# ScalarE writes the negated row maxima into the score banks ahead of the matmuls, in place of a fourth matmul pass

## The chip, the core and the metric

The kernel runs on one core of a Trainium2 chip. The metric is device time in microseconds (us), the median of three executions. The core has a TensorE (PE in the profile; PEld is its weight load), a VectorE (DVE), a ScalarE (ACT), a GpSimd (POOL) and a SyncE (SP), which here issues every DMA. Each engine works through its own instructions in program order and waits for the others through semaphores. Matmuls write into eight PSUM banks of 128 partitions by 512 fp32; VectorE and ScalarE read and write them as well.

## The reference

Four sequences of 1024 tokens, width 128, pass through half a mixture-of-experts FFN, an attention layer, and half the same FFN again:

```python
x = x + 0.5 * ffn(layernorm(x), ...)
x = x + attn(layernorm(x), ...)      # 16 heads of 64: q, k, v from two latents, rotary embedding,
                                     # softmax(q k^T / 8) v, output projection, residual
x = x + 0.5 * ffn(layernorm(x), ...)
```

The change touches the attention alone: for each query the scores against all 1024 keys, minus the query's largest score, go through an exponential.

## The kernel before

**Units.** The attention is cut into 64 units (`NUNIT`): two heads (`hh` is 0 or 1) by 512 queries each, 16 units to a sequence. The profile shows them as a stretch from 220 to 1457 us, one every 19 us or so. Inside a unit there are eight slots `s`, one for each tile of 128 keys. A score tile (`s`, `hh`) has the keys on the partitions and the 512 queries along the bank. The two heads lie on partitions 0 to 63 and 64 to 127, so that a matmul of one head runs beside a matmul of the other.

**Scores** (`score`, L938 and L942). Each tile is the sum of four matmuls `k`: high by high, high by low and low by high parts of K and Q, and as the last one `one_row` by `maxr`, an outer product that adds the negated maximum of each query, since the query lies along the bank and ScalarE's bias can't be used. Then ScalarE takes the exponential into `p` (L942) and GpSimd adds the tiles up for the denominator (`accumulate`, L954). Six banks go round: tile (`s`, `hh`) has bank number `(2*(s % 8) + hh) % 6` of psS0 to psS3, psC, psX.

**Maxima** (`passA`, L912 and L913). The maxima are taken 15 slots ahead from a single high-by-high product, 16 matmuls a unit into psA0 and psA1, each reduced by VectorE. `MAXIMA` says ahead of which score matmul of its head each of the first six pairs stands. `max_row` turns the 128x8 result into a row through DRAM: one DMA writes it, a second reads it back element by element into `maxr`, both on SP's queue.

**Order of a unit's program.** First `rows(0)` and `rows(1)`, interleaved one by one: 32 score matmuls of each head with the maxima between them, then the output projection of an earlier unit (`outp`, L997, a bank for each head: `bankO`) and the rotary step's three matmuls for each half (L797, banks `rope_banks`). After the rows, in this order:

- `scale`: ScalarE multiplies the two output banks by the reciprocal denominators, eight instructions (L1012).
- `den(U - 1)`: eight small matmuls (L974) and a ScalarE copy `dsb` (L976).
- `rope(U, "vector")`: VectorE's rotary arithmetic (L810 to L816); then the ScalarE casts to `hi_r` (L820).
- `add(1)` on VectorE: an output bank is added to X (L1006).
- `rope(U, "low")`: two VectorE subtractions (L823).
- `add(0)`, in the place "late": the other output bank.
- `values`: 32 matmuls into psC (L962), and the ScalarE copy `osb` (L965).

Between the values, `step(...)` runs pieces of the preparation of later blocks ("flows": the norms of coming attention blocks and of the second FFN, ScalarE's at L252, L691 and L695). After the values `step(PE)` may run a PE piece, such as the transposes L707 and L759 of a tile just normed, into psX (and in the first eight units a second one into psS3). Some forty of the 64 units have such pieces on ScalarE or PE. The next unit's scores begin behind them.

Rotary work runs nine units ahead (`NROPE`), so that units 55 to 63 have none.

Of the kernel before, what the change touches and what calls it, by code (L numbers as in the profile page):

```python
# [29 lines left out]
NGRP = NSLOT // 4  # L30
NUNIT = NSLOT // 8
PBUFS = 10
MAXIMA = ((2, 8, 13, 19, 24, 29), (0, 5, 11, 16, 21, 27))
OTHER, VECTOR, PE, NEVER, SCALAR, POOL = 0, 1, 2, 3, 4, 5
NROPE = 9
ACTS = (4, 6, 7)
# [11 lines left out]
class Kernel:  # L48
# [10 lines left out]
    def setup(self):  # L59
        nc, tc, ctx, ins = self.nc, self.tc, self.ctx, self.ins  # L60
        pool = lambda name, bufs, **k: ctx.enter_context(tc.tile_pool(name=name, bufs=bufs, **k))
        self.const = const = pool("const", 1)
        self.dram = pool("dram", 1, space=DRAM)
        self.small = pool("small", 2)
        self.prep = pool("prep", 1)

        bank = lambda name: pool(name, 1, space=PSUM).tile([128, 512], F32, name=name)
        self.psA, self.psS, self.psC, self.psX = [bank(f"ps_a{i}") for i in range(2)], [bank(f"ps_s{i}") for i in range(4)], bank("psc"), bank("psx")
        self.rest, self.nrest, self.slot, self.bankO = self.psA, 0, -NSLOT, None
        self.rope_banks = self.psA  # L70
# [12 lines left out]
        nc.scalar.activation(silu, silu, AF.Silu)  # L83
        self.consts = const.tile([128, 4], F32, name="consts")
        for i, c in enumerate((0.5, -CENTER, 1.0, EPS)):
            nc.gpsimd.memset(self.consts[:, i:i + 1], c)
        self.neghalf = const.tile([128, TPB], F32, name="neghalf")
        nc.gpsimd.memset(self.neghalf, -0.5)
        self.ones = const.tile([128, 32], F32, name="ones")
        nc.gpsimd.memset(self.ones, 1.0)  # L90

        self.one_row = const.tile([128, 128], F32R, name="one_row")
        nc.gpsimd.memset(self.f(self.one_row), 0.0)
        for hh in range(2):
            nc.gpsimd.memset(self.f(self.one_row[64 * hh:64 * hh + 1, :]), 1.0)
        self.maxr = [const.tile([128, 512], F32R, name=f"maxr{i}") for i in range(2)]
        for t in self.maxr:
            nc.gpsimd.memset(self.f(t), 0.0)

        self.table = const.tile([128, 3, S], F32, name="table")  # L100
# [818 lines left out]

    def max_row(self, U, m):  # L920
        nc = self.nc
        d = self.dram.tile([128, 8], F32, name=f"d3_{U % 4}")
        self.dma(out=d, in_=m)
        self.dma(out=self.maxr[U % 2][0:128:64, :].rearrange("h (q p) -> h q p", p=128), in_=d.rearrange("p (h q) -> h q p", h=2))

    def score(self, s, hh, k):


        nc = self.nc
        U, c = divmod(s, 8)  # L930
# [5 lines left out]
        ps = (self.psS + [self.psC, self.psX])[(2 * (s % 8) + hh) % 6]  # L936
        w, x = ((K[r, 0, ks], Q[r, 0, qs]), (K[r, 0, ks], Q[r, 1, qs]), (K[r, 1, ks], Q[r, 0, qs]), (self.one_row[r, :], self.maxr[U % 2][r, :]))[k]
        nc.tensor.matmul(ps, w, x, start=k == 0, stop=k == 3)  # L938
        if k == 3:
            if hh == 0:  # L940
                self.p_of[s] = self.pp.tile([128, 2, 512], F32, name="p")
            nc.scalar.activation(self.p_of[s][:, hh, :], ps, AF.Exp, scale=0.125)  # L942
            if hh == 1:
                self.accumulate(s)

    def accumulate(self, s):
# [20 lines left out]
    def den(self, U):  # L967

        nc = self.nc
        pd = self.psS[3]  # L970
        parts = [self.p_of[8 * U + c] for c in range(8 - direct(U), 8)] + [self.acc_of[U]]
        for k, part in enumerate(parts):
            for n in range(4):
                nc.tensor.matmul(pd[32 * n:32 * n + 32, 0:256], self.ones, part[:, n // 2, 256 * (n % 2):256 * (n % 2) + 256], start=k == 0, stop=k == len(parts) - 1)  # L974
        dsb = self.op1.tile([128, 256], F32, name="dsb")
        nc.scalar.copy(dsb, pd[:, 0:256])  # L976
        dT = self.ms.tile([128, 8], F32, name="dT")

        d1 = self.dram.tile([4, 256], F32, name=f"d1_{U % 4}")
        nc.sync.dma_start(out=d1, in_=dsb[0:128:32, :])  # L980
        g = 2 * U + 4
        self.at(g + (U == NUNIT - 1), lambda: nc.sync.dma_start(out=dT, in_=d1.rearrange("(h x) (y p) -> p (h x y)", x=2, p=128)), "mid")
        self.at(g + (2 if U == NUNIT - 1 else 1), lambda: self.outp(U, self.osb_of.pop(U), dT), "side")

    def outp(self, U, osb, dT):
# [8 lines left out]

        def mm(i, hh):
            r = slice(64 * hh, 64 * hh + 64)
            nc.tensor.matmul(po[hh][:, i * 128:(i + 1) * 128], osb[r, i * 128:(i + 1) * 128], self.G[r, j, :], start=True, stop=True)  # L997

        for hh in range(2):
            self.halves[hh] += [lambda i=i, hh=hh: mm(i, hh) for i in range(4)]  # L1000
# [11 lines left out]
                    nc.scalar.activation(po[hh][:, c], po[hh][:, c], AF.Identity, scale=rT[:, 4 * hh + i:4 * hh + i + 1])  # L1012

        self.at(self.group, scale, "scale")
        self.at(self.group, lambda: add(1))
        self.at(self.group, lambda: add(0), "late")

    def run(self):
        nc, tc = self.nc, self.tc
# [103 lines left out]
        for _ in streams[2].pop() if streams[2] else ():  # L1123
            pass
        assert not (streams[0] or streams[2])
        self.rest, self.rope_banks, self.bankO = [self.psX, self.psS[3]], self.psS[1:3], [self.psX, self.psS[0]]
        flows, needs, blocks = [], {}, list(range(1, B))
        self.attending = True

# [27 lines left out]
        for U in range(NUNIT):  # L1157
# [4 lines left out]

            def rows(hh):
                maxima = lambda i: self.passA(s0 + AHEAD + i, hh) if s0 + AHEAD + i < NSLOT else None
                for n in range(32):
                    if n in MAXIMA[hh]:
                        yield lambda n=n: maxima(MAXIMA[hh].index(n))
                    yield lambda n=n: self.score(s0 + n // 4, hh, n % 4)
                if hh == 1:
                    yield lambda: maxima(6)  # L1170
                for n, fn in enumerate(side[hh]):
                    if hh == 0 and n == 2:
                        yield lambda: maxima(6)
                    yield fn
                if hh == 0 and len(side[hh]) < 3:
                    yield lambda: maxima(6)
                yield lambda: maxima(7)

            for n, pair in enumerate(zip_longest(rows(0), rows(1))):
# [24 lines left out]
                if n == 32:  # L1204
# [32 lines left out]
        with ExitStack() as ctx:  # L1237
# [6 lines left out]
            g = self.ffn_pre(self.prep, (6, 7), x_of, self.wts2[:, 3].rearrange("p e t -> p t e"), rows=3)  # L1244

            def bg2(n):
                for place in ("mid", "side", "scale", "end", "late"):
# [62 lines left out]
```

## Time and profile before

| | us |
|---|---|
| median of 3 runs | 1624.37 (1622.91 to 1625.29) |
| profiled execution | 1621.56 |
| its span | 1619.7 |
| PE busy in the span | 1570.5 |
| POOL busy | 1378.8 |
| DVE busy | 1298.5 |
| ACT busy | 1115.2 |

The granted TensorE clock was 0.995. A group's row gives the line, the engine, what it writes and reads, the shape, the count, then the busy time and the mean duration of one in ns, and last the engine's idle time ahead of it. A row of the timeline gives the start, the length of a merged run, the engine and line, the count, and the idle time ahead of it with what ended it. Banks have no numbers there: psS0 to psS3 are all `ps_s`.

### The profile page before, as it was taken

The page shows a single profiled execution, that of the slowest core. Times are in us where ns is not written, and L with a number is a line of the kernel's source. Part 1 is how long each engine was busy: PE and PEld are TensorE (multiplying, and loading weights), DVE is VectorE, ACT ScalarE, POOL GpSimd, SP SyncE. Part 2 cuts the span into 40 slices and gives each one's busy share as a digit, 9 for nine tenths or more (in the row PEclk, how much of TensorE's full clock was granted, in tenths as well). Part 3 has the DMA queues.
Part 4 walks back from the last instruction along what each step waited for, and adds up shares of the span by engine and source line. Part 5 has one row for each costly group of instructions (what it writes and reads, how often), then busy time and mean ns, then how long its engine had stood idle before and what let it go on. Part 6 is the DMA issues. An engine that isn't in the chain of part 4 may idle for free.

```text
span 1619.7 us, 31073 instructions
## 1 busy us (share of the span) xinstructions
PE 1570.5 (97%) x10924; PEld 1054.0 (65%) x10924; DVE 1298.5 (80%) x2308; ACT 1115.2 (69%) x2488; POOL 1378.8 (85%) x820
## 2 busy tenths in 40 slices
PE   7998999999999999999999999999999999999998
PEld 5876766666666666566666666666666666556776
DVE  6566678898888889988888898889888866616897
ACT  4675667768777777777777777777677676665554
POOL 5678889989888889988989998989998898994676
PEclk9999999999999999999999999999999999999999
DMA  7025565565555555555555555655665532025543
GB/s 230 1 66 157 156 170 144 133 156 132 144 132 131 153 149 138 150 139 138 132 144 144 133 142 135 166 151 139 152 153 137 130 93 55 2 93 148 140 132 102
DMA packets 241148, 212.27 MB, mean 131 GB/s; under 512 B 157664, under 2 KB 170592, under 8 KB 240224
## 3 DMA queue, kind: packets, MB, share of 16 engines
q1 hardware_dynamic: 240992, 210.28, 50.0%
q8 instruction: 87, 1.43, 0.4%
q14 instruction: 69, 0.57, 0.1%
HBM read 130.39 MB, written 79.82 MB: 130 GB/s over the span
## 4 chain that ended last, share of the span: by engine, by line
PE 82%; DVE 6%; ACT 4%; POOL 3%; DMA 2%; issue 2%; SPq 1%; POOLq 0%; DVEq 0%; ACTq 0%
PE psc L962 25%; PE ps_s L938 21%; PE ps_a L912 8%; PE psc L938 4%; PE ps_s L463 3%; PE psx L938 3%; PE ps_s L543 3%; PE ps_s L797 2%; PE ps_s L997 2%; PE ps_s L974 2%; DVE m L913 2%; PE psx L498 2%; PE psc L434 1%; PE psx L997 1%; PE psc L543 1%
## 5 line engine op out<-in xcount | busy, mean ns | idle before, releaser
L954 POOL TENSOR_TENSOR acc<-acc,p 128x1024 f32<-128x1024 f32 x381 | 907.0, 2381 | 29.8
L913 DVE TENSOR_REDUCE m<-ps_a 128x1 f32<-128x512 f32 x1024 | 671.2, 685 | 161.9 <-PE ps_a L912 138.5
L942 ACT ACTIVATE p<-ps_s 128x512 f32<-128x512 f32 x768 | 411.5, 601 | 66.5 <-PE ps_s L938 42.7
L962 PE MATMUL psc<-p,ckn 128*64 128x512 f32 x2048 | 453.6, 595 | 0.0
L938 PE MATMUL ps_s<-QT,KT 64*128 64x512 f32 x2304 | 420.1, 394 | 0.3 <-DVE C_a L718 0.3
L912 PE MATMUL ps_a<-KT,QT 64*128 64x512 f32 x1024 | 390.1, 413 | 7.6 <-DVE m L913 5.8
L962 PEld LDWEIGHTS psc<-p,ckn 128*64 128x64 f32 x2048 | 141.4, 137 | 282.0 <-issue 282.0
L938 PEld LDWEIGHTS ps_s<-QT,KT 64*128 64x128 f32 x2304 | 284.3, 184 | 57.4 <-DVE X L1006 17.0
L954 POOL TENSOR_TENSOR acc<-p 128x1024 f32<-128x1024 f32 x64 | 153.8, 2403 | 86.8 <-ACT p L942 84.5
L912 PEld LDWEIGHTS ps_a<-KT,QT 64*128 64x128 f32 x1024 | 174.1, 184 | 43.4 <-DVE m L913 17.3
L938 PE MATMUL ps_s<-maxr,one_row 64*128 64x512 f32 x768 | 194.5, 392 | 0.0
L820 ACT CAST hi_r<-ps_s 128x512 fp32r<-128x512 f32 x110 | 64.5, 587 | 122.7 <-DVE ps_s L815 119.5
L938 PE MATMUL psx<-QT,KT 64*128 64x512 f32 x384 | 119.1, 390 | 0.0
L965 ACT COPY osb<-psc 128x512 f32<-128x512 f32 x64 | 37.3, 583 | 111.5 <-PE psc L962 111.5
L938 PE MATMUL psc<-QT,KT 64*128 64x512 f32 x384 | 109.2, 390 | 0.0
L938 PEld LDWEIGHTS ps_s<-maxr,one_row 64*128 64x128 f32 x768 | 102.4, 184 | 10.0
L551 POOL TENSOR_TENSOR p<-eo,p 128x512 fp32r<-128x512 f32 x42 | 62.7, 1499 | 41.5 <-ACT p L550 32.6
L1012 ACT ACTIVATE psx<-psx,rT 128x128 f32<-128x128 f32 x248 | 85.2, 344 | 17.5 <-ACT p L942 11.5
L447 POOL TENSOR_TENSOR X<-X,dtmp 128x512 f32<-128x512 f32 x54 | 69.2, 1281 | 31.7 <-ACT dtmp L446 30.6
L1012 ACT ACTIVATE ps_s<-ps_s,rT 128x128 f32<-128x128 f32 x248 | 84.3, 340 | 6.0
L942 ACT ACTIVATE p<-psc 128x512 f32<-128x512 f32 x128 | 77.4, 605 | 6.7 <-PE ps_a L912 3.3
L942 ACT ACTIVATE p<-psx 128x512 f32<-128x512 f32 x128 | 77.9, 608 | 0.0
(268 smaller groups left out, 2664.0 us busy)
## 6 DMA issues: line engine op xcount, KB each, us to landing
C_l<-cs SPq DMA_DIRECT2D x128, 256.0 KB
QT<-qs SPq DMA_DIRECT2D x256, 128.0 KB
KT<-ks SPq DMA_DIRECT2D x256, 128.0 KB
qs<-hi_r SPq DMA_DIRECT2D x32, 512.0 KB
qs<-eo SPq DMA_DIRECT2D x32, 512.0 KB
ks<-hi_r SPq DMA_DIRECT2D x32, 512.0 KB
ks<-eo SPq DMA_DIRECT2D x32, 512.0 KB
rt<-wt SPq DMA_DIRECT2D x52, 256.0 KB
```

What stands on the lines that cost most here:

```text
L447: nc.gpsimd.tensor_tensor(X[:, t:t + 4, :], X[:, t:t + 4, :], tmp, ALU.add)
L463: nc.tensor.matmul(p, w[:, a, e, :], xs[:, c, :], start=k == 0, stop=k == 2)
L543: nc.tensor.matmul(p, w[:, a, e, :], xs[:, c, :], start=k == 0, stop=k == 2)
L551: (nc.gpsimd if m < N - 1 else nc.vector).tensor_tensor(sh[:, 1, :], hp, self.f(sh[:, 0, :]), ALU.subtract)
L820: nc.scalar.copy(w["hi"][:, k, :], w["ps"][k])
L912: nc.tensor.matmul(self.psA[hh], self.QT[P % 3][r, 0, q0:q0 + 128], self.KT[P % 3][r, 0, kk * 512:kk * 512 + 512], start=True, stop=True)
L913: nc.vector.tensor_reduce(m[0][:, hh, qb, kk:kk + 1], self.psA[hh], AX.X, ALU.max)
L938: nc.tensor.matmul(ps, w, x, start=k == 0, stop=k == 3)
L942: nc.scalar.activation(self.p_of[s][:, hh, :], ps, AF.Exp, scale=0.125)
L954: nc.gpsimd.tensor_tensor(acc, self.p_of[s - 1] if c == 1 else acc, self.p_of[s], ALU.add)
L962: nc.tensor.matmul(self.psC[64 * hh:64 * hh + 64, :], self.ckn[b % 2][:, c, :], self.p_of[s][:, hh, :], start=c == 0, stop=c == 7)
L1012: nc.scalar.activation(po[hh][:, c], po[hh][:, c], AF.Identity, scale=rT[:, 4 * hh + i:4 * hh + i + 1])
```

## The change

Three parts belong together.

1. `max_row` writes the row to DRAM already transposed (two rows of 512), reads it into `maxr` with contiguous rows, and, from unit 1 on, also reads it broadcast over all 128 partitions into a new tile `maxb` (512 KB).
2. At the end of each unit, behind `rope(U, "low")`, `fill(U + 1)` has ScalarE copy `maxb` into the banks of the next unit's tiles (0, 0), (0, 1), (1, 0), and, from unit 9 on, (1, 1). These tiles then have three matmuls, the first of which adds to the bank; the fourth is left out. `MAXIMA` is dealt anew for the shorter rows.
3. Banks: the output projection goes from psX and psS0 to psS0 and psS1, the rotary step from psS1 and psS2 to psS2 and psS3, the denominator from psS3 to psX. Both adds now stand ahead of `rope(U, "low")`. In an output bank only the first of four quarter matmuls has the start flag.

```diff
-MAXIMA = ((2, 8, 13, 19, 24, 29), (0, 5, 11, 16, 21, 27))
+MAXIMA = ((2, 7, 13, 18, 23, 28), (0, 5, 10, 15, 20, 25))
...
     def max_row(self, U, m):
         nc = self.nc
-        d = self.dram.tile([128, 8], F32, name=f"d3_{U % 4}")
-        self.dma(out=d, in_=m)
-        self.dma(out=self.maxr[U % 2][0:128:64, :].rearrange("h (q p) -> h q p", p=128), in_=d.rearrange("p (h q) -> h q p", h=2))
+        d = self.dram.tile([2, 512], F32, name=f"d3_{U % 4}")
+        self.dma(out=d.rearrange("h (q p) -> p h q", p=128), in_=m.rearrange("p (h q) -> p h q", h=2))
+        self.dma(out=self.maxr[U % 2][0:128:64, :], in_=d)
+        if U:
+            self.nc.sync.dma_start(out=self.maxb.rearrange("p h q -> p (h q)"), in_=d.rearrange("h q -> (h q)").unsqueeze(0).to_broadcast([128, 1024]))
+
+    def bank(self, s, hh):
+        return (self.psS + [self.psC, self.psX])[(2 * (s % 8) + hh) % 6]
+
+    def fill(self, U):
+        for s, hh in ((0, 0), (0, 1), (1, 0)) + (((1, 1),) if U > 8 else ()):
+            self.nc.scalar.copy(self.bank(s, hh), self.maxb[:, hh, :])
+            self.filled.add((8 * U + s, hh))
...
-        nc.tensor.matmul(ps, w, x, start=k == 0, stop=k == 3)
-        if k == 3:
-            if hh == 0:
+        nc.tensor.matmul(ps, w, x, start=k == 0 and not filled, stop=k == last, skip_group_check=filled)
+        if k == last:
+            second = s in self.p_of
+            if not second:
...
-        pd = self.psS[3]
+        pd = self.psX
...
-            nc.tensor.matmul(po[hh][:, i * 128:(i + 1) * 128], osb[r, i * 128:(i + 1) * 128], self.G[r, j, :], start=True, stop=True)
+            nc.tensor.matmul(po[hh][:, i * 128:(i + 1) * 128], osb[r, i * 128:(i + 1) * 128], self.G[r, j, :], start=i == 0, stop=True, skip_group_check=i > 0)
...
-        self.at(self.group, lambda: add(1))
-        self.at(self.group, lambda: add(0), "late")
+        self.at(self.group, lambda: [add(hh) for hh in range(2)])
...
-        self.rest, self.rope_banks, self.bankO = [self.psX, self.psS[3]], self.psS[1:3], [self.psX, self.psS[0]]
+        self.rest, self.rope_banks, self.bankO = [self.psX, self.psS[3]], self.psS[2:4], self.psS[0:2]
...
             rope(U, "low")
-            self.run_later(2 * U + 1, "late")
+            if U + 1 < NUNIT:
+                self.fill(U + 1)
             rope(U, "end")
```

More of the change, by code (lines that the diff above doesn't have):

```diff
@@ L98, in setup @@
             nc.gpsimd.memset(self.f(t), 0.0)
+        self.maxb = const.tile([128, 2, 512], F32, name="maxb")
+        self.filled = set()
         self.table = const.tile([128, 3, S], F32, name="table")
@@ L935, in score @@
         Q, K = self.QT[P % 3], self.KT[P % 3]
-        ps = (self.psS + [self.psC, self.psX])[(2 * (s % 8) + hh) % 6]
+        ps = self.bank(s, hh)
+        filled = (s, hh) in self.filled
+        last = 2 if filled else 3
         w, x = ((K[r, 0, ks], Q[r, 0, qs]), (K[r, 0, ks], Q[r, 1, qs]), (K[r, 1, ks], Q[r, 0, qs]), (self.one_row[r, :], self.maxr[U % 2][r, :]))[k]
-        nc.tensor.matmul(ps, w, x, start=k == 0, stop=k == 3)
-        if k == 3:
-            if hh == 0:
+        nc.tensor.matmul(ps, w, x, start=k == 0 and not filled, stop=k == last, skip_group_check=filled)
+        if k == last:
+            second = s in self.p_of
+            if not second:
                 self.p_of[s] = self.pp.tile([128, 2, 512], F32, name="p")
             nc.scalar.activation(self.p_of[s][:, hh, :], ps, AF.Exp, scale=0.125)
-            if hh == 1:
+            if second:
                 self.accumulate(s)
@@ L1164, in rows @@
                 maxima = lambda i: self.passA(s0 + AHEAD + i, hh) if s0 + AHEAD + i < NSLOT else None
-                for n in range(32):
+                steps = [(s, k) for s in range(s0, s0 + 8) for k in range(3 if (s, hh) in self.filled else 4)]
+                for n, (s, k) in enumerate(steps):
                     if n in MAXIMA[hh]:
                         yield lambda n=n: maxima(MAXIMA[hh].index(n))
-                    yield lambda n=n: self.score(s0 + n // 4, hh, n % 4)
+                    yield lambda s=s, k=k: self.score(s, hh, k)
                 if hh == 1:
@@ L1203, in run @@
                     self.run_later(2 * U + 1, "mid")
-                if n == 32:
+                if n == 31:
                     self.run_later(2 * U + 1, "side")
@@ L1246, in bg2 @@
             def bg2(n):
-                for place in ("mid", "side", "scale", "end", "late"):
+                for place in ("mid", "side", "scale", "end"):
                     self.run_later(NGRP + 1 + n, place)
```

## The prediction

> **What bounds the kernel now.** I read the page first: busy shares, then the chain that ended last, then the groups.
>
> ```profile
> PE 1570.5 (97%) x10924; PEld 1054.0 (65%) x10924; DVE 1298.5 (80%) x2308; ACT 1115.2 (69%) x2488; POOL 1378.8 (85%) x820
> ...
> PE 82%; DVE 6%; ACT 4%; POOL 3%; DMA 2%; issue 2%; SPq 1%; POOLq 0%; DVEq 0%; ACTq 0%
> ...
> L938 PE MATMUL ps_s<-maxr,one_row 64*128 64x512 f32 x768 | 194.5, 392 | 0.0
> ...
> L965 ACT COPY osb<-psc 128x512 f32<-128x512 f32 x64 | 37.3, 583 | 111.5 <-PE psc L962 111.5
> ```
>
> PE bounds the span, and the maxima matmuls to be cut stand on it. ScalarE idles for 111.5 us ahead of `osb`: the tail of a unit, where the fills go. So I read that tail in the timeline, engine by engine, in a unit without flow pieces:
>
> ```profile
> 1182.32 2.24 ACT L942 ACTIVATE p<-ps_s 128x512 f32<-128x512 f32 x4
> ...
> 1187.50 0.38 ACT L976 COPY dsb<-ps_s 128x256 f32<-128x256 f32 x1
> 1190.01 1.19 ACT L820 CAST hi_r<-ps_s 128x512 fp32r<-128x512 f32 x2 [2.13 <-DVE ps_s L815]
> 1193.22 0.59 ACT L965 COPY osb<-psc 128x512 f32<-128x512 f32 x1 [2.03 <-PE psc L962]
> 1194.61 1.09 ACT L942 ACTIVATE p<-ps_s 128x512 f32<-128x512 f32 x2 [0.81 <-PE ps_s L938]
> ...
> 1190.48 0.68 DVE L1006 TENSOR_TENSOR X<-ps_s,X 128x512 f32<-128x512 f32 x1
> 1191.08 1.28 DVE L823 TENSOR_TENSOR eo<-ps_s,hi_r 128x512 fp32r<-128x512 f32 x2
> 1192.27 0.68 DVE L1006 TENSOR_TENSOR X<-psx,X 128x512 f32<-128x512 f32 x1
> ...
> 1183.22 0.27 PE L997 MATMUL psx<-G,osb 64*128 64x128 f32 x1
> ...
> 1184.40 0.95 PE L797 MATMUL ps_s<-C_l,wup 64*128 64x512 f32 x6
> ...
> 1186.09 7.09 PE L962 MATMUL psc<-p,ckn 128*64 128x512 f32 x32
> 1193.10 0.50 PE L938 MATMUL ps_s<-QT,KT 64*128 64x512 f32 x1
> ```
>
> See three things. PE goes from values to the next scores without a gap (call that moment E, 1193.10). VectorE's tail ends at E - 0.15, close to it. The rotary matmuls (L797) start 0.16 us before the last exponential ends (1182.32 + 2.24 = 1184.56): their banks were read by earlier ones. Last, a unit with a flow piece:
>
> ```profile
> 1057.34 1.65 ACT L252 ACTIVATE yf<-X,rstdf 128x128 f32<-128x128 f32 x4
> 1059.47 0.59 ACT L965 COPY osb<-psc 128x512 f32<-128x512 f32 x1 [0.48 <-PE psc L962]
> ...
> 1059.35 0.66 PE L759 MATMUL psx<-ident,yf 128*128 128x128 f32 x4
> 1059.94 0.49 PE L938 MATMUL ps_s<-QT,KT 64*128 64x512 f32 x1
> ```
>
> ScalarE norms a tile right behind the casts, from E - 2.02, and PE transposes it at E = 1059.35, with no wait.
>
> **The change part by part.**
>
> *Matmuls removed.* Pairs of score matmuls start every 0.23 us (1193.44, 1193.68, ... 1194.14, 1194.37 in the timeline). Four tiles less one matmul are two pairs, 0.46 us a unit from unit 9 on; three tiles shorten the longer head's row by one, 0.23 us in units 1 to 8. In all 8 x 0.23 + 55 x 0.46 = 27 us of PE work.
>
> *What of it stays: the banks dealt anew.* Exponentials follow each other every 0.48 us, 16 make 7.7 against 8.4 of PE, so ScalarE keeps up and everything up to the last exponential moves earlier by 0.46. But the second rotary bank is now psS3, which that last exponential reads. It ends at 1184.56 - 0.46 = 1184.10; with 0.07 for the signal (the casts start 0.04 after L815 ends; I allow a little more) PE may go at 1184.17, where it wanted 1184.40 - 0.46 = 1183.94. So 0.23 of 0.46 is lost in that wait, and behind it on PE stand the last maxima, the denominator and the values. Bounds: nothing lost, all lost. The output banks cost nothing: psS1 is read two exponentials earlier, 0.48 and 0.66 apart, so it is free at 1184.10 - 1.14 = 1182.96 and needed at 1183.47 - 0.46 = 1183.01. In units 1 to 8 the same wait takes the whole 0.23. In units 4, 10, 18, 25, 30, 34, 39, 43, 53 and 57 a VectorE subtraction of a flow (0.68, L718 or L762) stands among the reductions, the projection starts 9.3 us after the scores in place of 8.6, and PE waits there for reductions: no gain. Units 55 to 63 have no rotary step and keep 0.46. Sum: 38 x 0.23 + 8 x 0.46 = 12.4 us gained.
>
> *The fills.* No row has an SBUF to PSUM copy; the nearest, `osb` at 0.583 and the 256-wide `dsb` at 0.38, bound it from below; above, the 0.68 of VectorE's pass over a bank. I take 0.59, with 0.48 to the next start. 244 of them add 144 us to ScalarE (1115 to 1259 of some 1630): not the bound by share. Place decides. VectorE's tail is now add, add, low, low, ending at E - 1.95, -1.35, -0.75, -0.15. Each fill waits for one of these, so the four start at E - 1.92, -1.31, -0.71 and -0.11, the last ending at E + 0.48. Without flow pieces that is free: slot 1's scores come at E + 0.92; `osb` starts at E + 0.37 for 0.05 and psC is needed at E + 1.9; the first exponential can start at E + 0.85, its tile is ready at E + 1.2. In units 55 to 63 the adds are done by E - 4, and nothing waits.
>
> *Flow pieces queued behind the fills.* This is the cost. In units with rotary work, ScalarE's norms can start only after the last fill: E + 0.37 in place of E - 2.02, so 2.39 later (1.79 with three fills, up to unit 7). Read from the timeline at each unit's end:
> - Units 29, 38, 42, 52: four norms, 0.39 apart, now end at E + 2.0. PE's last transpose and the scores come 0.3 later, E + 2.3 where it was E + 0.58: 1.72 each, 6.9.
> - Units 8, 11, 23, 26: nine ScalarE instructions ran to E + 1.5 and PE waited already (L707); the whole shift is added, 4 x 2.39 = 9.6.
> - Units 2, 22, 3: shorter pieces, 1.2 + 1.0 + 0.4 = 2.6.
> - Units 9 and 24 (norms ahead of the casts L716 and L717 that free psX): 0.8 each; 21: `osb` and so psC 0.95 late; 7: 0.4; 20: 0.15. Together 3.1.
> - The others carry two small instructions or none, inside the 0.35 of slack.
> Sum 22.2. Bounds: 11 if half of it finds slack that I don't see, 29 if the four units of the first line pay the full shift and the others somewhat more.
>
> *The DMAs.* One more issue a unit on SP (0.42 to 0.58 a row), 63 x 512 KB = 33 MB to the 212 moved; DMA engines half busy. The element-wise side moves from the read to the write. As a read its 1,024 packets of 4 bytes ran from 1009.1 to 1012.8, 3.7 us, and held up the issue behind it (`qs<-hi_r` 3.75 against 0.46 for `qs<-eo`); now SP waits as long for the write before it issues both reads, and the queued stores and K/Q loads come no later. In the tighter unit the write was issued at 1025.2, so it ends near 1031, and the broadcast near 1035; the first fill wants it at 1038.7. Cost nil, with 3.7 us of cover; each us beyond costs about that in every second unit.
>
> The Trainium skill speaks against this part: "DMA: Bandwidth & Descriptors", Specifications, puts line rate at 512 bytes and more and has smaller transfers read, modify and write. If that doubled the 3.7 us, an estimate, the broadcast would still land about when it is wanted, and the sum would stand. No row here shows such a write.
>
> The skill also speaks against the idea: "PSUM — Partial Sum Buffer", The four PSUM rules, would put any seed but zero through PE, which is what the kernel before does, since a write by ScalarE doesn't set the bits by which a matmul adds or overwrites. By that rule the seed stays on PE with its 27 us, no fill stands in ScalarE's queue, and the sum is no change. No row here shows an addition to a bank that ScalarE wrote.
>
> *Else.* Denominator in psX: free since slot 5, nothing. POOL needs 17.1 us a unit, below 18.5, nothing.
>
> *Sum.* 22.2 - 12.4 = +9.8 us on the profiled 1621.6 (its span 1619.7 and 1.9 around it): 1631.4. The median of the runs lies 2.8 above that execution; on it, 1634.2.
>
> **The rivals.**
> - *The gain comes through whole:* no wait in the rotary step. Then 8 x 0.23 + 38 x 0.46 + 3.7 = 23.0 against 22.2: 1623.6, no change. For: the wait is 0.23 us, worked out from modelled matmul ends. Against: bank and order are in the program.
> - *The flow pieces find room (other side):* if their delay costs under 12.4 - 3.2 = 9.2 us, the kernel is faster; at 5 it is 1617. Place: ScalarE between the casts and `osb`. For: it idles 2.03 there in most units. Against: that idle time ends at the fills, which wait for VectorE until E - 0.1.
> - *A further wait:* the broadcast lands late, or reductions, now every 1.37 us a pair for VectorE's 1.3, hold PE. A late landing by 1 us in every second unit, less 0.5 of slack, or 0.4 a unit for reductions: some 13 to 25 more, 1648 to 1659.
>
> **How the numbers follow.** Forecast 0.62, whole gain 0.10, room 0.15, further wait 0.13. Bounds of the two sums give +9.8 with -9 and +18 for the forecast's own ends; the range cuts these to 1619 to 1647, which holds the forecast and half of the room case. The measurement tells 0.2% (3.2 us) from no change. Faster 0.15; same 0.10; slower 0.75.
>
> **What would show it.** Right: the maxima group on `ps_s` at 524 in place of 768; in a plain unit the rotary matmuls waiting some 0.2 us for `p` L942, a period 0.2 us shorter; ScalarE's fills at E - 1.9 to E + 0.5; `psx` L759 and L707 waiting about 2 us for L252 in eight units. Wrong: periods shorter by 0.46, PE without those waits, or fills waiting for a DMA.

## The result, and the profile after

The changed kernel takes 1961.36 us (median of 4 runs, 1951.76 to 1967.38) against 1623.64 for the kernel before on the same chip: a ratio of 1.208, 95% interval 1.202 to 1.213. The prediction said 1634.2, at most 1647. The sign was right; the size, 338 us against 9.8, was wrong by a factor of 34. The profiled execution took 1960.35 us, its span is 1958.6.

First the page of the changed kernel: busy time, the granted clock in 40 slices (tenths), the chain that ended last by engine and by line, and three groups (busy us, mean ns of one, idle time ahead and its releaser).

```profile
PE 1679.1 (86%) x10680; PEld 1111.8 (57%) x10680; DVE 1314.6 (67%) x2308; ACT 1233.2 (63%) x2732; POOL 1375.2 (70%) x820
...
PEclk9899989998889888899888989998998889999999
...
PE 34%; DMA 34%; ACT 9%; SPq 7%; DVE 5%; issue 4%; POOL 2%; POOLq 0%; ACTq 0%; DVEq 0%; another core or an unknown queue 0%
DMA dT<-d 9%; DMA d<-m 9%; PE ps_s L952 9%; SPq L57 7%; PE psc L977 6%; DMA ks<-hi_r 4%; DMA qs<-hi_r 4%; DMA KT<-ks 4%; PE ps_a L914 4%; ACT ps_s L935 2%; PE ps_s L545 2%; ACT ps_s L1027 2%; DVE m L915 2%; PE ps_s L1012 2%; PE psc L952 2%
...
L935 ACT COPY ps_s<-maxb 128x512 f32<-128x512 f32 x244 | 134.4, 598 | 36.8 <-DMA maxb<-d 34.4
L952 PE MATMUL ps_s<-maxr,one_row 64*128 64x512 f32 x524 | 156.7, 394 | 0.0
...
L1008 DVE RECIPROCAL rT<-dT 128x8 f32<-128x8 f32 x64 | 12.6, 197 | 124.6 <-DMA dT<-d 124.6
```

The edit itself did what it says: 524 maxima matmuls in place of 768, 244 copies of 0.598 us. But no engine bounds the kernel any more. PE went from 97% to 86% of the span, and the chain, which was 82% PE and 2% DMA, is now 34% PE and 34% DMA. The two DMAs at its head, `d<-m` and `dT<-d`, carry 4 KB each. A reciprocal of 0.2 us waits 124.6 us in total for one of them.

So I asked what SP's queue waits for. The row gives total us, times, longest us. First the kernel before, then the changed one:

```profile
SPq L57 <- DMA d<-m: 146.1, 64, 4.7
```

```profile
SPq L57 <- DMA d<-m: 630.6, 64, 12.1
```

SP issues the read of the row only when the store `d<-m` has landed. That took 146.1 / 64 = 2.3 us of standing still, and now takes 9.9 us, 64 times. From the trace, from the issue of the store to the last of its completions, the median went from 2.7 to 10.5 us. Some waits of the other engines in the changed kernel:

```profile
...
PEld ps_a L914 <- DVE m L915: 142.1, 76, 7.4
ACT hi_r L822 <- DMA ks<-hi_r: 125.2, 24, 8.5
DVE rT L1008 <- DMA dT<-d: 124.6, 28, 16.9
...
PE ps_a L914 <- DVE m L915: 120.7, 48, 7.2
ACT hi_r L822 <- DMA qs<-hi_r: 112.1, 21, 9.4
PEld ps_s L952 <- ACT ps_s L935: 104.3, 83, 5.3
...
ACT ps_s L935 <- DMA maxb<-d: 34.4, 9, 7.0
```

In the kernel before, the first and the third of these were:

```profile
PEld ps_a L912 <- DVE m L913: 17.3, 37, 1.1
...
DVE rT L993 <- DMA dT<-d: 13.6, 4, 9.9
```

One unit of the changed kernel shows how a late transfer reaches PE (timeline: start, length, engine, line, and in brackets the idle time ahead and its releaser):

```profile
1409.18 0.42 SPq L997 DMA_DIRECT2D dT<-d  x1
1409.70 0.53 SPq L57 DMA_DIRECT2D d<-m  x1
1420.50 0.52 SPq L57 DMA_DIRECT2D maxr<-d  x1
...
1421.51 0.43 SPq L57 DMA_DIRECT2D ks<-hi_r  x1
...
1409.88 3.46 DVE L915 TENSOR_REDUCE m<-ps_a 128x1 f32<-128x512 f32 x5 [0.20 <-PE ps_a L914]
1419.47 0.20 DVE L1008 RECIPROCAL rT<-dT 128x8 f32<-128x8 f32 x1 [6.13 <-DMA dT<-d]
...
1420.28 0.79 PE L914 MATMUL ps_a<-KT,QT 64*128 64x512 f32 x1 [6.06 <-DVE m L915]
```

Two transfers are late here. `dT`, issued half a microsecond before the element-wise store, arrives 10.3 us later, where 3.9 is usual. VectorE has the reciprocal in its queue ahead of the next reduction, so the maxima matmul, and with it PE, stands still for 6 us. And the stores of the rotary halves (`ks<-hi_r`), which stand behind the row's read in SP's queue, go out 11.8 us after its issue (2.1 to 4.9 in units 48 to 53 of the kernel before); ScalarE's next casts into that tile wait for them, and the fills and the next scores wait behind the casts. By the packet records, the store's 1,024 packets have all started by 1414, but it lands at 1420.4; between 1414 and 1420 no DMA packet of any queue runs.

Not every unit loses. PE stands still for over 3 us in 27 of the 64 units, for 7.9 us at most; in the kernel before it never does for 1.5. In places the loss alternates: by the timeline, from the end of one unit's values to the end of the next, units 49, 51 and 53 took 13.4 to 13.7 us more than before, units 50, 52 and 54 between 0.1 and 0.25 less. The attention stretch (end of the first unit's values to end of the last one's) grew from 1217.0 to 1550.3 us: 333 of the 339 us by which the span grew.

Part of it is the clock. The granted clock fell from 0.995 to 0.923, and PE's busy time grew by 109 us though it has 244 matmuls less. After a standstill of 1.9 us pairs of score matmuls started every 0.43 us for a while (1405.15, 1405.58, 1406.00), where 0.23 is usual; the granted clock from 1405.0 to 1408.0 was 0.50 to 0.52. So about a third of the loss, as an estimate from those 109 us, is PE running more slowly after it was made to wait.

### The profile page after: what moved, and what is told of

It reads as the page before. It is cut to its first block, busy times and chain, and to the rows that moved or that the text cites. A ratio compares the mean times of both kernels' runs of the same rounds, so it can differ in the third digit from the quotient of the medians.

```text
span 1958.6 us, 30813 instructions
## 1 busy us (share of the span) xinstructions
PE 1679.1 (86%) x10680; PEld 1111.8 (57%) x10680; DVE 1314.6 (67%) x2308; ACT 1233.2 (63%) x2732; POOL 1375.2 (70%) x820
## 4 chain that ended last, share of the span: by engine, by line
PE 34%; DMA 34%; ACT 9%; SPq 7%; DVE 5%; issue 4%; POOL 2%; POOLq 0%; ACTq 0%; DVEq 0%; another core or an unknown queue 0%
DMA dT<-d 9%; DMA d<-m 9%; PE ps_s L952 9%; SPq L57 7%; PE psc L977 6%; DMA ks<-hi_r 4%; DMA qs<-hi_r 4%; DMA KT<-ks 4%; PE ps_a L914 4%; ACT ps_s L935 2%; PE ps_s L545 2%; ACT ps_s L1027 2%; DVE m L915 2%; PE ps_s L1012 2%; PE psc L952 2%
## 5 line engine op out<-in xcount | busy, mean ns | idle before, releaser
L952 PE MATMUL ps_s<-QT,KT 64*128 64x512 f32 x2304 | 483.1, 429 | 66.8 <-ACT ps_s L935 66.0
L914 PE MATMUL ps_a<-KT,QT 64*128 64x512 f32 x1024 | 425.2, 449 | 122.4 <-DVE m L915 120.7
L952 PEld LDWEIGHTS ps_s<-QT,KT 64*128 64x128 f32 x2304 | 331.9, 203 | 142.8 <-ACT ps_s L935 104.3
L1027 ACT ACTIVATE ps_s<-ps_s,rT 128x128 f32<-128x128 f32 x496 | 164.5, 341 | 172.9 <-PE ps_s L1012 121.3
L935 ACT COPY ps_s<-maxb 128x512 f32<-128x512 f32 x244 | 134.4, 598 | 36.8 <-DMA maxb<-d 34.4
L952 PE MATMUL ps_s<-maxr,one_row 64*128 64x512 f32 x524 | 156.7, 394 | 0.0
L825 DVE TENSOR_TENSOR eo<-ps_s,hi_r 128x512 fp32r<-128x512 f32 x110 | 70.7, 684 | 83.9 <-ACT hi_r L822 77.4
L1012 PE MATMUL ps_s<-G,osb 64*128 64x128 f32 x992 | 109.2, 304 | 0.5 <-ACT p L957 0.5
L1012 PEld LDWEIGHTS ps_s<-G,osb 64*128 64x128 f32 x992 | 100.6, 208 | 3.5 <-ACT p L957 1.4
L1021 DVE TENSOR_TENSOR X<-ps_s,X 128x512 f32<-128x512 f32 x124 | 85.1, 686 | 17.4 <-ACT ps_s L1027 10.9
L1008 DVE RECIPROCAL rT<-dT 128x8 f32<-128x8 f32 x64 | 12.6, 197 | 124.6 <-DMA dT<-d 124.6
```

The source lines that it names most:

```text
L825: nc.vector.tensor_tensor(w["eo"][:, k, :].bitcast(F32R), w["ps"][k], self.f(w["hi"][:, k, :]), ALU.subtract)
L914: nc.tensor.matmul(self.psA[hh], self.QT[P % 3][r, 0, q0:q0 + 128], self.KT[P % 3][r, 0, kk * 512:kk * 512 + 512], start=True, stop=True)
L935: self.nc.scalar.copy(self.bank(s, hh), self.maxb[:, hh, :])
L952: nc.tensor.matmul(ps, w, x, start=k == 0 and not filled, stop=k == last, skip_group_check=filled)
L1021: nc.vector.tensor_tensor(x, po[hh].rearrange("p (t d) -> p t d", t=4), x, ALU.add)
```

## The experiments

In the order in which they ran; "stretch" is the growth of the attention stretch of 1217.0 us in the profiled execution. Each ratio is against the kernel before on the same chip, where its medians were 1621.9 to 1623.6.

| kernel | what | median us | ratio, 95% | stretch |
|---|---|---|---|---|
| changed | | 1961.36 | 1.202 to 1.213 | +333.3 |
| e1 | before + element-wise store | 1879.93 | 1.156 to 1.161 | +262.5 |
| e2 | row from SBUF, second DRAM row | 1759.15 | 1.083 to 1.086 | +134.2 |
| e3 | no transposition | 1655.27 | 1.019 to 1.021 | +30.5 |
| e4 | e2, no fill behind 17 units | 1705.72 | 1.049 to 1.054 | +76.3 |
| e5 | row turned on PE | 1687.28 | 1.037 to 1.042 | +63.4 |
| e6 | e5, no fill behind 20 units | 1652.07 | 1.016 to 1.021 | +32.7 |
| e7 | e1, read later | 1931.18 | 1.187 to 1.193 | +308.5 |
| e8 | before + turn | 1645.69 | 1.012 to 1.015 | +21.6 |
| e9 | e8 + three fills | 1642.78 | 1.010 to 1.014 | +20.0 |
| e10 | e3, no fill behind 20 units | 1623.99 | 0.999 to 1.001 | -1.7 |
| e11 | e8, turn in two halves | 1648.41 | 1.014 to 1.017 | +25.6 |
| e12 | e11 + four fills | 1637.76 | 1.007 to 1.011 | +15.5 |
| e13 | e7, store on ScalarE's queue | 1858.74 | 1.143 to 1.148 | +235.9 |
| e14 | e11, turn in the scores' type | 1648.15 | 1.014 to 1.017 | +24.2 |
| e15 | e14 + fills, other banks | 1642.49 | 1.011 to 1.013 | +17.5 |

### The element-wise store: e1, e3, e2

**e1** puts only the store and the contiguous read of the change into the kernel before: no broadcast, no fills, no banks.

```diff
-        d = self.dram.tile([128, 8], F32, name=f"d3_{U % 4}")
-        self.dma(out=d, in_=m)
-        self.dma(out=self.maxr[U % 2][0:128:64, :].rearrange("h (q p) -> h q p", p=128), in_=d.rearrange("p (h q) -> h q p", h=2))
+        d = self.dram.tile([2, 512], F32, name=f"d3_{U % 4}")
+        self.dma(out=d.rearrange("h (q p) -> p h q", p=128), in_=m.rearrange("p (h q) -> p h q", h=2))
+        self.dma(out=self.maxr[U % 2][0:128:64, :], in_=d)
```

> The kernel before with only the element-wise store of the maxima row and the contiguous read; no broadcast, no fills, banks and matmuls as before. In the changed kernel the read of the row follows its store on SP's queue by 10.5 us (median of 64) where it was 2.8. Theory S (the slow store holds SP's queue, and the stores, loads and row reads behind it come late): nearly the whole loss is here, 1880 to 1960 us. Theory B (the 33 MB of broadcast make all transfers late): 1620 to 1640. Theory F (PE waits for the fills themselves): 1620 to 1640.

Measured: 1879.93 us. SP's wait and three waits of engines in e1:

```profile
SPq L57 <- DMA d<-m: 659.7, 64, 12.1
```

```profile
DVE rT L993 <- DMA dT<-d: 171.4, 32, 10.8
PE ps_a L912 <- DVE m L913: 169.5, 57, 9.3
...
ACT hi_r L820 <- DMA ks<-hi_r: 47.9, 11, 8.1
```

The same waits as in the changed kernel, with nothing of the fills in it. The store and the read behind it cost 258 us by themselves.

**e3** keeps the whole change but stores the maxima as they lie.

```diff
-        self.dma(out=d.rearrange("h (q p) -> p h q", p=128), in_=m.rearrange("p (h q) -> p h q", h=2))
+        self.dma(out=d.rearrange("h (r c) -> (h r) c", c=8), in_=m)
```

> The changed kernel with the maxima stored to DRAM as they lie, 32 bytes a partition, so that no DMA of the row goes element by element; it leaves out the transposition, and each query gets another query's maximum. Theory S: 1625 to 1640, a little under e2 since the element-wise read is gone too. Theory B and theory F: 1850 or more.

Measured: 1655.27 us, 306 less than the changed kernel; SP waits for the store as in the kernel before:

```profile
SPq L57 <- DMA d<-m: 124.4, 64, 4.7
```

This settles two things. The store explains all but 32 us of the loss, alone or together with what it delays. And the broadcast, 63 transfers of 512 KB, costs nothing that can be seen: plain units are shorter than before (below). Between e1's 258 and these 306 us lie some 50 us that belong to fills and broadcast meeting a late row; I have not taken them apart.

**e2** avoids the element-wise store in another way: store and read as before, then the finished row goes from `maxr` to a second DRAM row, and the broadcast comes from there.

```diff
+            d2 = self.dram.tile([2, 512], F32, name=f"d4_{U % 4}")
+            self.at(self.group, lambda: self.dma(out=d2, in_=self.maxr[U % 2][0:128:64, :]), "end")
+            self.at(self.group + 1, lambda: self.nc.sync.dma_start(out=self.maxb.rearrange("p h q -> p (h q)"), in_=d2.rearrange("h q -> (h q)").unsqueeze(0).to_broadcast([128, 1024])), "mid")
```

> The changed kernel with the row stored and read element by element as before the change; a second contiguous DRAM row is written from maxr eight score matmuls later, and the broadcast into maxb is read from that, another nine later. Fills, banks and broadcast all stay. Theory S: 1628 to 1640, the prediction's own sum for fills and banks (+9.8). Theory B and theory F: 1850 or more, as the broadcast and the fills are still there.

Measured: 1759.15 us. The store is quick again, but a chain of four transfers in one unit brings the broadcast too late:

```profile
ACT ps_s L937 <- DMA maxb<-d: 129.8, 45, 10.0
```

That is the rival "a further wait", met in a kernel of my own. **e4** is e2 without fills behind 17 units that carry flow pieces (`if U + 1 < NUNIT and U not in FLOWS`).

> e2 with no fill at the end of the 17 units in which ScalarE has norms of a flow behind it (1, 2, 3, 7, 8, 9, 11, 20 to 24, 26, 29, 38, 42, 52); their successors have four matmuls a tile. If flow pieces queued behind the fills cost 22 us, as predicted, and a fill is worth 0.23 us to its unit, this is about 18 us under e2. If they find room, it is 0 to 6 us above e2, by the matmuls that come back.

Measured: 1705.72, 53 us less, far more than the flow pieces alone were said to cost. Each fill left out also takes a wait for the late broadcast with it, so e4 doesn't isolate the flow pieces; e10 does.

### Why the neighbours are late: e7, e13

Two readings were open after e1: SP stands still behind the store, or the store delays what else is moving. **e7** is e1 with the row's read issued 17 matmuls later, so that SP can go on.

```diff
-        self.dma(out=self.maxr[U % 2][0:128:64, :], in_=d)
+        read = lambda: self.dma(out=self.maxr[U % 2][0:128:64, :], in_=d)
+        self.at(self.group + 1, read, "mid") if U else read()
```

> The kernel before with the element-wise store of the first experiment (1880), but with the read of the row issued 17 score matmuls later, so that SP issues the stores of the rotary step and other DMAs in between and does not stand still for the store's landing. Theory Q (SP's in-order wait makes all that is behind it late): 1624 to 1660. Theory D (the writes themselves slow the transfers beside them, the denominators' dT above all): 1750 to 1880, with VectorE's wait for dT still some 170 us.

Measured: 1931.18 us, 51 us slower than e1 and above both theories' figures. SP's wait fell by two fifths (VectorE's for `dT` from 171.4 to 78.0):

```profile
SPq L57 <- DMA d<-m: 389.7, 51, 11.8
```

But what SP now issues right behind the store lands with it. From issue to last completion, `qs<-hi_r` took a median of 13.0 us (5.9 in the kernel before), `qs<-eo` 13.1 (4.4), and the store itself 12.2. So SP's standstill is only a part: the store slows transfers that are in flight beside it, before it (`dT`) and behind it.

**e13** asks whether that goes by the queue: e7 with the store issued from ScalarE's queue.

```diff
-        self.dma(out=d.rearrange("h (q p) -> p h q", p=128), in_=m.rearrange("p (h q) -> p h q", h=2))
+        (nc.scalar if U else nc.sync).dma_start(out=d.rearrange("h (q p) -> p h q", p=128), in_=m.rearrange("p (h q) -> p h q", h=2).bitcast(F32))
```

> e7 (the kernel before with the element-wise store, the row read 17 matmuls later) with that store issued from ScalarE's DMA queue in place of SP's. Theory 1 (transfers issued behind it on the same queue land with it, and those of other queues do not): SP's qs stores and dT reads land in 5 to 6 us again, 1640 us or less. Theory 2 (the store holds up what other queues move as well, in the DMA engines or at the memory): about as e7, above 1850 us.

Measured: 1858.74 us. The transfers of SP's queue are better, not well: `qs<-hi_r` has a median of 4.6 us but a tenth of them take over 13.7; for `dT` a tenth takes over 12.0 (4.7 before). SP waits again, since the read comes before the store has landed:

```profile
SPq L57 <- DMA d<-m: 618.3, 59, 16.6
```

So the delay reaches another queue's transfers; but as SP's wait came back too, e13 doesn't say how much of the 236 us is the one and how much the other. The packet records show the others being held: of the packets of 2 KB that started 1 to 12 us after a store's issue, 18% took over 1 us in e7 and 8% in e13, where the store's own packets have a queue of their own; the longest took 9.6 and 8.9 us. In the kernel before their median is 0.084 us and the longest 1.3. Why a store of 1,024 elements, whose packets are recorded at 0.009 us each, holds the others up stays open.

### The flow pieces: e10, e5, e6

**e10** is e3 without fills behind 20 units (`U not in COSTLY`: 0 to 3, 7 to 9, 11, 20 to 24, 26, 29, 31, 38, 42, 44, 52).

> e3 (the changed kernel with the maxima stored as they lie, which leaves out the transposition of the row) without fills behind the same 20 units. Theory 1 (what e3 is slower than before is the flow pieces queued behind the fills, some 38 us by the periods): that goes, and with it the gain of up to 0.23 us a unit in the 20 units; the rotary wait of 0.2 stays there: 1617 to 1626 us, at the kernel before. Theory 2 (the banks dealt anew, or the broadcast of 33 MB, cost something everywhere): 1640 or more.

Measured: 1623.99 us, a ratio of 0.999 to 1.001. The 31 us are the fills behind these 20 units, which were picked because e3 was slower there; that the cost is the flow pieces behind the fills is read from the timelines. Without them the change is worth nothing: plain units are 0.2 us shorter than before, most of the units without fills up to 0.47 longer (0.88 behind unit 0).

e3's timeline has both the tail that the prediction drew and the piece that it priced. A plain unit (E is 1210.54) and the end of unit 29, each with PE and ScalarE:

```profile
1201.64 1.16 PE L799 MATMUL ps_s<-C_l,wup 64*128 64x512 f32 x6
...
1210.54 0.49 PE L952 MATMUL ps_s<-QT,KT 64*128 64x512 f32 x1
...
1208.44 0.59 ACT L935 COPY ps_s<-maxb 128x512 f32<-128x512 f32 x1
1209.24 1.79 ACT L935 COPY ps_s<-maxb 128x512 f32<-128x512 f32 x3 [0.20 <-DVE X L1021]
1210.96 0.58 ACT L980 COPY osb<-psc 128x512 f32<-128x512 f32 x1
```

```profile
836.41 1.48 PE L761 MATMUL psx<-ident,yf 128*128 128x128 f32 x4 [0.89 <-ACT yf L254]
837.83 0.50 PE L952 MATMUL ps_s<-QT,KT 64*128 64x512 f32 x1
...
834.15 1.79 ACT L935 COPY ps_s<-maxb 128x512 f32<-128x512 f32 x3 [0.21 <-DVE X L1021]
835.87 1.64 ACT L254 ACTIVATE yf<-X,rstdf 128x128 f32<-128x128 f32 x4
```

In the plain unit the rotary group takes 1.16 us in place of 0.95: the wait for psS3. The fills run from E - 2.1 to E + 0.49. In unit 29 the norms start only behind the fills, PE waits 0.89 us for the first of them and then goes at their pace, one every 0.39 us.

**e5** gives the changed kernel a transposition without the element-wise store: PE turns the 128x8 maxima into psC, VectorE copies, eight pieces of 512 bytes are stored, and row and broadcast are read from them.

```diff
+        nc.tensor.transpose(self.psC[0:8, 0:128], self.f(m8), self.ident)
+        mT = self.ms.tile([8, 128], F32, name="mT")
+        nc.vector.tensor_copy(mT, self.psC[0:8, 0:128])
+        d = self.dram.tile([8, 128], F32, name=f"d4_{U % 4}")
+        nc.sync.dma_start(out=d, in_=mT)
+        self.dma(out=self.maxr[U % 2][0:128:64, :], in_=d.rearrange("(h q) p -> h (q p)", h=2))
```

> The changed kernel with the maxima turned into a row on chip: PE transposes the 128x8 maxima into psC between the last uses of that bank in a unit, VectorE copies the 8x128 result, one DMA stores it as eight runs of 512 bytes, and the row read and the broadcast follow; no DMA of the row goes element by element. All fills stay. If the element-wise transfers alone made the difference between the changed kernel and the run without a transposition (1655), this gives 1650 to 1662, and ScalarE's wait for maxb is near nothing. If the broadcast is late once it starts 9 us into the unit, 1680 or more, with that wait in the list.

**e6** is e5 without fills behind the 20 units.

> The same with no fill at the end of the 20 units (0 to 3, 7, 8, 9, 11, 20 to 24, 26, 29, 31, 38, 42, 44, 52) behind which the run without a transposition was slower than the kernel before, by 38 us together. If that loss is the flow pieces that queue behind the fills, it goes away whole and the other units keep 0.2 us each (0.4 from unit 55 on): 1612 to 1619, faster than the kernel before. If the delay comes with the fills wherever they stand, 1625 or more.

Measured: 1687.28 and 1652.07. ScalarE's wait for `maxb` is 12.6 us in e5, too little for the 32 us that e5 lies above e3. The fills behind the 20 units cost 35 us here, 31 in e3; what is left, 28 us from e10 to e6 or some 0.45 us a unit, came with the turn.

### The price of the turn: e8, e11, e14

**e8** is the kernel before with the turn alone, two pairs of scores later than in e5.

> The kernel before with the turned row alone: its 128x8 maxima are transposed by PE into psC, copied by VectorE and stored with eight descriptors of 512 bytes; no broadcast, no fills, banks as before. The transpose stands two pairs of scores later than in e5. Theory 1 (the 0.4 us a unit that the turn cost in e5 was PE waiting for the exponential of slot 5 in psC, 0.36 of it): the wait is gone, at most 0.1 us a unit is left, 1622 to 1632 us. Theory 2 (the turn itself costs, through VectorE's copy among the reductions or the store): 0.3 to 0.4 us a unit, 1642 to 1650.

Measured: 1645.69 us, 0.35 us a unit; theory 1 falls. e8's timeline on PE around the turn:

```profile
1181.64 0.39 PE L953 MATMUL ps_s<-QT,KT 64*128 64x512 f32 x1
1181.96 0.27 PE L933 MATMUL psc<-ident,m 128*8 128x128 f32 x1
1182.16 0.73 PE L953 MATMUL ps_s<-QT,KT 64*128 64x512 f32 x4
1182.73 0.40 PE L953 MATMUL ps_s<-maxr,one_row 64*128 64x512 f32 x2
```

From 1181.64 to 1182.73 there are three steps of scores, 0.69 us at the usual 0.23, and they take 1.09. The waits put it down to an exponential, but both exponentials of slot 5 had ended by 1181.60. Over all units of e8, e11 and e14 the turn starts 0.32 us behind the matmul ahead of it (median of each), while its distance to the last exponential's end ranges from 0.05 to 0.53: so it follows PE's own stream, not the exponentials. **e11** therefore turns in two half-height matmuls 15 pairs earlier, ScalarE copying:

```diff
+        for r in (slice(0, 64), slice(64, 128)):
+            nc.tensor.matmul(self.psC[r.start:r.start + 8, 0:64], self.f(m8)[r, :], self.ident[r, r], start=True, stop=True)
+        mT = self.ms.tile([72, 64], F32, name="mT")
+        nc.scalar.copy(mT, self.psC[0:72, 0:64])
```

> e8 with the turn done otherwise: two matmuls of half height (64 partitions each) against the identity into psC, in place of one transpose of full height; ScalarE copies the result in place of VectorE; two stores of 256-byte pieces; and it stands 15 pairs of scores earlier. No broadcast, no fills. Theory 1 (the 0.35 us a unit in e8 is PE going from weights of half height to one of full height and back: 0.86 us from the pair ahead of the turn to the second pair behind it, where two steps take 0.46): at most 0.15 a unit is left, 1622 to 1633 us. Theory 2 (PE waits for an exponential in psC, or the copy and the store cost): as e8, 1640 or more.

**e14** makes it one matmul with operands of the scores' type:

```diff
+        nc.tensor.matmul(self.psC[0:8, 0:128], m8, self.identr, start=True, stop=True)
+        mT = self.ms.tile([8, 128], F32, name="mT")
+        nc.scalar.copy(mT, self.psC[0:8, 0:128])
```

> e11 with the turn as one matmul of full height whose operands have the type F32R of the scores around it (the maxima have it already; a copy of the identity gets it), in place of two of half height in F32; one store of 512-byte pieces. No broadcast, no fills. Theory 1 (PE loses its 0.4 us a unit in going from F32R matmuls to F32 ones and back): one step of 0.1 to 0.2 us is left, 1625 to 1637 us. Theory 2 (any small matmul that stands among the scores breaks their stride): 0.35 to 0.4 us a unit as in e8 and e11, 1644 to 1650.

Measured: 1648.41 and 1648.15, 0.40 us a unit both. Changing height, type, place and copying engine didn't help: a small matmul among the score pairs costs 0.35 to 0.40 us, though its own record is 0.22 to 0.27. Which property breaks the stride stays open; all the forms load 8 weight columns where the scores load 128, and no run varied that.

### What the fills can bring: e9, e12, e15

**e9** adds the broadcast and three fills to e8, on the banks of the kernel before, not behind the 20 units.

```diff
+        for s, hh in ((0, 0), (0, 1), (1, 0)):
+            self.nc.scalar.copy(self.bank(s, hh), self.maxb[:, hh, :])
+            self.filled.add((8 * U + s, hh))
...
+            if U + 1 < NUNIT and U not in COSTLY:
+                self.fill(U + 1)
```

> e8 with the broadcast and three fills, (0, 0), (0, 1) and (1, 0), on the banks of the kernel before (the rotary step stays on psS1 and psS2, so that its matmuls need not wait for the last exponential), and no fill behind the 20 units that e6 skips. Theory 1 (the fill idea is sound where no flow piece stands behind it): one pair of score matmuls less in 43 units, 43 x 0.23 = 10 us below e8, 1612 to 1622, no slower than before. Theory 2 (a fill in the tail makes PE wait somewhere even in a unit without flow pieces, or the broadcast collides with other transfers): at e8 or above it.

Measured: 1642.78 us, 3 us below e8 and inside the spread of the two. Plain units gain 0.02 us, not 0.23: one pair less brings nothing there. That the maxima, dealt for rows of 32, then wait for reductions is argued from the timeline alone.

**e12** is e11 with four fills, still on the banks of before, and the maxima dealt as in the changed kernel.

```diff
+        for s, hh in (((1, 1),) if U > 8 else ()) + ((0, 0), (0, 1), (1, 0)):
```

> e11 with the broadcast and the fills of the changed kernel (four from unit 9 on) on the banks of the kernel before, where the rotary step does not touch the bank of the last exponential; no fill behind the 20 units that e6 skips; the maxima dealt as in the changed kernel. Theory 1 (in a unit without flow pieces the fills are free, and without the rotary wait the whole 0.46 us comes through): 40 x 0.46 less some 4 us for units in which PE waits for reductions, 14 us below e11, 1608 to 1618, faster than before. Theory 2 (VectorE's sixteen reductions, 10.4 us a unit, hold PE once the row of scores is shorter, as in e9, where the one pair saved brought only 0.02 a unit): less than 5 us below e11.

Measured: 1637.76 us, 10.7 below e11, between the two theories. Here tile (1, 1) doesn't get the reference's sum: its bank psS3 was last written by the denominator, in half of its columns only. I take it that in the other half the matmuls overwrite the fill; no run shows that by itself, but it fits the Trainium skill, "PSUM — Partial Sum Buffer", The four PSUM rules, by which ScalarE's write leaves untouched the bits that decide between adding and overwriting, and it would be why the change moved the denominator to psX. PE's work is the same, and its time is what counts here: in plain units the period falls by some 0.4 us from e11 to e12 (unit 14: 19.21 to 18.77). **e15** moves the fourth fill to tile (2, 1) in psX, behind the values and only where no flow piece used psX.

```diff
+            if U + 1 < NUNIT and U not in COSTLY and not flow:
+                self.fill(U + 1, ((2, 1),))
```

> e14 with the broadcast and the fills, on the banks of the kernel before: (0, 0), (0, 1) and (1, 0) behind the low subtractions, and (2, 1) in psX behind the values where no flow piece took psX, in place of (1, 1), whose bank the denominator fills only to half in this layout. No fill behind the 20 units that e6 skips; the maxima dealt as in the changed kernel. Theory 1 (as in e12, where the plain units lost 0.43 us of period, the whole 0.46 comes through without the rotary wait): some 30 units x 0.43 and 10 x 0.2, 14 us below e14; if e14 is at 1630 that is 1616, faster than before. Theory 2 (the fill of psX behind the values makes the scores of slot 0 or 2 wait for ScalarE): less than 6 us below e14.

Measured: 1642.49 us, 5.7 below e14, at the edge of theory 2's figure. Plain units again gain some 0.4 (unit 14: 19.19 to 18.75), and the rotary group runs without a wait:

```profile
1221.16 0.96 PE L802 MATMUL ps_s<-C_l,wup 64*128 64x512 f32 x6
```

But only the units with all four fills gain. Where three remain, unit 31 for one, the period stays (20.19 to 20.13), and units without a fill lose up to 0.2 more. The turn's 25 us is never earned back. No version here beats the kernel before; the nearest, e10, leaves out the transposition and ends level with it.

## Why the prediction was wrong

**The DMAs: "Cost nil". This is the step that failed.** It took the element-wise write to last as long as the element-wise read, 3.7 us: issued at 1025.2, it should end near 1031, 5.8 us from issue to landing, with cover up to 1038.7. The write takes 10.5 us (by the same measure the read had taken 4.8), so SP's queue is held some 7.6 us longer in every unit (630.6 - 146.1 over 64), and the step's other half, that queued stores and K/Q loads "come no later", fell with it. A price was carried from one direction of transfer to the other with no row that showed it.

It also asked only who waits for the row itself: the first fill. On its own times a write of 10.5 us brings the broadcast about 1 us too late, and the fills do wait only 34.4 us for it, a tenth of the loss. The larger losses came from transfers that have nothing to do with the row but share the path, `dT` and the rotary stores.

The Trainium skill, "DMA: Bandwidth & Descriptors", Specifications, has transfers under 512 bytes read, modify and write. That was a warning, but no price: pieces of 32 bytes are under 512 as well and landed in 2.7 us, and no run here shows what the 4-byte store does at the memory. The estimate of a doubling that I drew from it was too small, and said nothing of the neighbours.

**Flow pieces: right in kind, mis-sized.** 22.2 us, bounds 11 to 29; in e3 the units that got longer add up to 38, and the others gained 7.5. Of the 38, 6 stay in e10, where no fill stands behind these units; the fills account for 31 to 32. Three terms were short. Units 8, 11, 23 and 26 cost 3.7 each, not 2.4 less the 0.2 gained. The units 31 and 44, whose ScalarE pieces come from routing, were overlooked: 2.4 and 3.7. So was unit 1, 0.86 against 0.29 in e10; the 0.86 behind unit 0 is there in e10 too, so it isn't the fill's. The four units of the first line were right: their scores come at E + 2.36, predicted E + 2.3, and the period grows by 1.2 to 2.0 us against 1.72 - 0.23.

**The fills and the rotary wait: right.** 0.598 us each against 0.59; E - 2.1 to E + 0.49 against E - 1.92 to E + 0.48; no cost in plain units. There 0.2 of 0.46 us came through (predicted 0.23), and 0.2 to 0.43 in units 55 and later (predicted 0.46). e12 and e15, with the rotary banks left alone, bring some 0.4, and their rotary group runs without the wait, so the missing half was lost in the wait for psS3.

**The sum.** With the DMA step right, the prediction would have been about e3: 1655 us, not 1634; the flow pieces alone put it outside the range.

**The rivals.** "Whole gain" and "room" fell with e3. "A further wait" named the right family, but priced a late broadcast at 13 to 25 us. In the changed kernel the fills wait 34.4 us for it, in nine units; the waits that count stand elsewhere. Fills waiting for a DMA was one of the prediction's own signs of being wrong. The case without a seed by ScalarE didn't come: the matmuls add to what ScalarE wrote, and e5 and e15, with fills of that kind, give the reference's output; e12, whose fourth bank was written in half of its columns, doesn't.

## What to carry to other kernels

When a transposition moves from a DMA's read to its write, price the new direction by a run of that transfer alone, and then ask what else is in flight beside it: a 4 KB store in each unit cost 258 us in a kernel whose engines were all within their budgets. An engine's in-order queue makes any insertion a delay for everything behind it, so count every unit's pieces, not the plain unit. And one small matmul between regular pairs can cost more than its own length.

## What the runs showed of the hardware

- A store of 1,024 elements of 4 bytes from 128 partitions to DRAM took 10.5 us to land; the same 4 KB in 128 pieces of 32 bytes took 2.7. Transfers issued next to it took 9 to 13 us where 4 to 6 is usual, some of those on another queue too; single packets of 2 KB took up to 9.6 us where 0.084 is the median.
- With PE standing still for over 3 us in 27 of 64 units (7.9 at most), the granted clock over the run was 0.923, where it was 0.995 without; e1, with such standstills in 25 units, had 0.946, and e3, with none over 2.8 us, 0.989.
- A transpose of 128x8, itself 0.22 to 0.27 us on PE, cost 0.35 to 0.40 us a unit amid score matmuls, in three forms (e8, e11, e14).
- Matmuls without the start flag added to banks that ScalarE had filled (e5, 244 fills; e15).
- A ScalarE copy of 128x512 from SBUF into a PSUM bank took 0.598 us; the one from PSUM to SBUF 0.58.
